# A block-matching convolution kernel: cosine transform on sixteen 32x32 tiles, its loads in pieces over the slots, products behind six multiply-adds, and another slot for layer 1's matmuls

## The chip, the cores and the metric

The kernel runs on one core of a Trainium2 chip. The metric is the device time of one execution in microseconds (us); less is better. In the profiles PE is TensorE's matmul side and PEld its weight loads, DVE is VectorE, ACT is ScalarE, POOL is GpSimd, and SP is the engine whose queue issues some of the DMAs. PSUM is the memory that matmuls write to, in banks of 128 partitions by 512 floats.

## The reference

The input is `x`, 8 images of 32 channels by 128x128 in float32. Two layers follow each other; `_gn` normalises over groups of channels.

```python
# layer 0, on x0 = _gn(x)
xb = _patch_match_stack(x0)      # for each pixel the 8 best of 25 shifts of x0
                                 # (5x5 window, 3x3 patch costs, top_k): [B, 256, H, W]
dct = _conv(xb, dct_w, groups=C) # 1x1, per channel 8 -> 8 maps: the "cosine transform"
h = jax.nn.relu(_conv(_conv(xb, w1), w2, groups=CK, pad=1))  # 1x1 over 256, 3x3 depthwise
h = jax.nn.relu(_conv(_conv(h, w3), w4, groups=CK, pad=1))
wiener = jax.nn.sigmoid(_conv(_conv(h, w5), w6, groups=CK, pad=1))
filt = _conv(wiener * dct, inv_dct_w, groups=C)
x = x + _conv(filt, agg_w)       # 256 -> 32
# layer 1: one 5x5 kernel for all channels
x = x + conv5x5(_gn(x), kernel)
```

The 256 maps are held as two tensors of 128 partitions by 8 rows by 128 columns. The inverse transform and `agg_w` are one matmul in the kernel (`pa`).

## The kernel before, in words

**Steps and slots.** An image is cut into 17 steps of up to 8 rows; the 8 images make 136 steps in one long pipeline. The main loop (L1056 on) goes through four *slots* a step, `i` = 3, 2, 1, 0. Slot `i` = 1, 2, 3 runs the i-th of layer 0's three "1x1, then 3x3 depthwise" blocks, each for another step (`si = s - (i - 1)`, block 3 two steps behind block 1). Slot 0 ends a step: the cosine transform, and its products with the sigmoid's result.

**A block.** Half of the 256 maps goes the "v" way and half the "t" way. `pointwise_v` (L658) multiplies 128-row groups into PSUM tiles `pv` (matmul L670), ScalarE copies them to `tv`. `depthwise_v` (L711) then makes the 3x3 convolution on DVE: ScalarE writes the first tap (L722), DVE does eight multiply-adds (L725), each 128x1024, and ScalarE the relu or the sigmoid (L729). `pointwise_t` (L680; matmuls `p`, L694; copies L701) and `depthwise_t` (matmuls `pw`, L751, ScalarE L764) do the same for the other half on TensorE, with the taps as banded matrices.

**The gather.** The 8 shifted copies of a pixel are gathered by matmuls: POOL loads the chosen places `ib` (L602) and the image's rows `xt` (L591), ScalarE turns the places into selection matrices `sel` (L616, L617), and TensorE multiplies (`gather_pixels`, `pg`, L631). ScalarE copies the result to `xb` (L638), the input of block 1. Each slot gathers a quarter of the step. After the last quarter of a step, POOL stores all of `xb` to DRAM as `xbd` (one DMA of 1 MB, L640), since the transform needs it two steps later.

**The end of a step.** `final_load` (L770), called at the end of slot 0 for the next step, has POOL load the input's rows `xr` (L781) and the stored maps `xf` (eight DMAs, L791). `final_dct` (L796) runs in slot 0: per half of the 8 rows, four matmuls of 64x64 tiles `pc` (L810) into two PSUM tiles, and two products on DVE, `acc = acc * pc` (L818). `ldct`, the weights of the transform, is made once at the start by `mixes` (L300): SP loads `dq` by 32 small DMAs (L308), and DVE multiplies it by a mask (L318). `final_add` (L820) follows in slot 0 and the next step's slot 3: matmuls `pa` (L831), an addition on DVE (L839), statistics (L840), and four POOL stores to `x1d` (L844).

**The other work.** While image b runs through the pipeline, image b+1 is prepared (patch costs: differences `df` L444, squares on ScalarE L452, sums over channels `pd` on TensorE L459, POOL's stores and loads `sq` L474 and `dsum` L492/L499, sums on DVE from L508 on, the eight best places by `mx` and `idx` L536/L537; the gather's table: `xl` L411, then `xtd`, 32 POOL stores L424/L429), and image b-1 goes through layer 1 (`layer1` L848: `xy` loads, normalisation, matmuls `p` of the 5x5 bands L924, additions L936, stores L938). These tasks are generators. Each `yield` names a queue (D: DVE, B, A, P: TensorE matmuls, Q), a cost and a number of slots to wait; the main loop calls `run("P")`, `run("Q")`, `run("A")` at fixed places of each slot, and `tick` runs D with a credit, 40% of a step's in slot 0 and 20% in each of the others.

**What sets the order.** The order of TensorE, DVE and ScalarE is written by hand: instructions run on each of them as the loop issues them (`manual_schedule`). The order on POOL and SP is the framework's, so an edit can move POOL's DMAs beyond what its lines say. `ps_x` holds five PSUM banks that `pv`, `p`, `pg`, `pc`, `pa`, `p` of layer 1 and others take in turn; `pd` and `pw` have pools of their own. `xf` has one buffer.

**The iterators of the main loop.** `depthwise_v` is a generator: its first part is ScalarE's first tap, its second the eight multiply-adds (`next(new_v)`, in the block's own slot), its third the activation (`next(dv)`, in the slot after it), its last the copy of the two overlapping rows (`next(kept)`, two slots later). `dt` goes through `depthwise_t` likewise. Slot 0 comes after block 1's slot 1, so on DVE the products L818 stand behind block 1's eight multiply-adds.

Of the kernel before, what the change touches and what calls it, by code (L numbers as in the profile page):

```python
# [16 lines left out]
P = 128  # L17
# [3 lines left out]
R = 8  # L21
# [23 lines left out]
def bm3d_conv_preact(  # L45
# [58 lines left out]
    lw5 = const.tile([P, 2, CK], F32, name="lw5")  # L104


    ldct = const.tile([P, 2, 64], F32, name="ldct")
    lagg = const.tile([P, 2, C], F32, name="lagg")


# [90 lines left out]

    queues = {"B": deque(), "D": deque(), "A": deque(), "P": deque(), "Q": deque()}

    PAIR = 1.95
    pairs = [0]
# [91 lines left out]

    def mixes():  # L300

        dq = work.tile([P, 2, K], F32, name="dq", tag="dq", bufs=1)
        src = dct_w.rearrange("(m h c i) k a b -> m h k c (i a b)", m=2, h=2, i=K)
        for k in range(K):
            for m in range(2):
                for h in range(2):
                    p = 64 * h + 32 * (k % 2) + 8 * (k // 2)
                    nc.sync.dma_start(dq[p : p + 8, m], src[m, (h + m + 1) % 2, k])  # L308
        m8 = work.tile([P, 8], F32, name="m8", tag="m16", bufs=1)
        yield "D", 1.0, 10  # L310
        nc.vector.tensor_reduce(
            m8,
            cst[:, C_M32 : C_M32 + C].rearrange("p (a c) -> p c a", c=8),
            axis=mybir.AxisListType.X,
            op=ALU.add,
        )
        for m in range(2):
            nc.vector.tensor_tensor(  # L318
                ldct[:, m].rearrange("p (c i) -> p c i", i=K),
                m8.unsqueeze(2).to_broadcast([P, 8, K]),  # L320
                dq[:, m].unsqueeze(1).to_broadcast([P, 8, K]),
                ALU.mult,
            )

        iv = work.tile([P, 2, K], F32, name="iv", tag="iv", bufs=1)
        nc.sync.dma_start(iv, inv_w.rearrange("(m p) k a b -> p m (k a b)", p=P))
        ag = work.tile([C, CK], F32, name="ag", tag="xr")
        nc.sync.dma_start(ag, agg_w.rearrange("c i a b -> c (i a b)"))
        for m in range(2):
            yield "D", 0.5  # L330
            ib = work.tile([P, P], F32, name=f"ib_{m}", tag="xm")
            nc.vector.tensor_tensor(
                ib.rearrange("p (c k) -> p c k", k=K),
                cst[:, C_M16 : C_M16 + 16].unsqueeze(2).to_broadcast([P, 16, K]),
                iv[:, m].unsqueeze(1).to_broadcast([P, 16, K]),
                ALU.mult,
            )
            yield "P", 0
            ps = ps_x.tile([P, 512], F32, name=f"ps_ag_{m}", tag="x")[:, :C]
            nc.tensor.transpose(ps, ag[:, m * P : (m + 1) * P], ident[:C, :C])  # L340
            agt = work.tile([P, C], F32, name=f"agt_{m}", tag="agt")
            nc.scalar.copy(agt, ps)
            yield "P", 0
            ps2 = ps_x.tile([P, 512], F32, name=f"ps_ia_{m}", tag="x")[:, :C]
            nc.tensor.matmul(ps2, ib, agt, start=True, stop=True)
            nc.scalar.copy(lagg[:, m], ps2)
# [273 lines left out]
    def gather_pixels(b, s4, f):  # L620

        n, h = s4 // 2, s4 % 2
        if h == 0 and f == 0:
            xbs[b, n] = xbp.tile([P, 2, R, W], F32, name=f"xb_{b}_{n}", tag="xb")
        xb, xt = xbs[b, n], xts[b, s4]
        sels = [selss.pop((b, s4, f, k2)) for k2 in range(2)]
        pg = ps_x.tile([P, 2, 4, HW], F32, name=f"pg_{b}_{s4}_{f}", tag="x")
        for t in range(NT // 2):
            xa, xz = TW * t, min(TW * (t + 1), HW)
            for j in range(4):  # L630
                nc.tensor.matmul(  # L631
                    pg[C * j : C * (j + 1), :, :, xa:xz],
                    xt[: 8 * QW, f * (NT // 2) + t],
                    sels[j // 2][: 8 * QW, j % 2 * 2 : j % 2 * 2 + 2, :, xa:xz],
                    start=True,
                    stop=True,
                )
        nc.scalar.copy(xb[:, :, 4 * h : 4 * h + 4, HW * f : HW * (f + 1)], pg)  # L638
        if h == 1 and f == 1:
            nc.gpsimd.dma_start(xbd[b][:, :, R * n : R * (n + 1)], xb)  # L640

# [67 lines left out]
    def depthwise_v(i, b, n):  # L711
        v = tv[i - 1]
        nr = R if n < NS else i
        out_ = accp.tile([P, R, W], F32, name=f"acc{i}_{b}_{n}_1", tag=f"acc{i}1")
        acc = out_[:, :nr]
        for k, (dy, dx) in enumerate(
            ((1, 1), (0, 0), (0, 1), (0, 2), (1, 0), (1, 2), (2, 0), (2, 1), (2, 2))
        ):
            tap = dwv[:, i - 1, 3 * dy + dx : 3 * dy + dx + 1]
            rows = v[:, dy : dy + nr, dx : dx + W]  # L720
            if k == 0:
                nc.scalar.activation(acc, rows, AF.Copy, scale=tap)  # L722
                yield out_
            else:
                nc.vector.scalar_tensor_tensor(  # L725
                    acc, rows, tap, acc, op0=ALU.mult, op1=ALU.add
                )
        yield
        nc.scalar.activation(acc, acc, funcs[i - 1])  # L729
        yield  # L730
        rows_before_v(i, b, n)
# [38 lines left out]
    def final_load(b, n):  # L770
        j0, j1 = (3, R) if n == 0 else (0, R if n < NS else 3)
        ya, yz = R * n - 3 + j0, R * n - 3 + j1

        whole = j1 - j0 == R
        nr, nw = (2, W) if whole else (j1 - j0, C)
        xr = work.tile([P, 2 * W], F32, name=f"xr_{b}_{n}", tag="xr")
        xr = xr[:, : nr * nw].rearrange("p (r w) -> p r w", w=nw)
        for j in range(4):
            ra = ya + 2 * j if whole else ya
            xa = 0 if whole else C * j  # L780
            nc.gpsimd.dma_start(  # L781
                xr[C * j : C * (j + 1)], x[b, :, ra : ra + nr, xa : xa + nw]
            )

        xf = xbp.tile([P, 2, R, W], F32, name=f"xf_{b}_{n}", tag="xf", bufs=1)
        src = xbd[b].rearrange("(j m h c) g y x -> g m h j c y x", j=4, m=2, h=2)
        for m in range(2):
            for h in range(2):
                for g in range(2):
                    p = 64 * h + C * g  # L790
                    nc.gpsimd.dma_start(  # L791
                        xf[p : p + C, m, j0:j1], src[g, m, (h + m + 1) % 2, :, :, ya:yz]
                    )
        return xr, xf, j0, j1

    def final_dct(b, n, acc, xf, j0, j1):  # L796

        for r0 in range(0, R, 4):
            a, z = max(r0, j0), min(r0 + 4, j1)
            if a >= z:  # L800
                continue


            pc = [
                ps_x.tile([P, 4, W], F32, name=f"pc_{b}_{n}_{m}_{r0}", tag="x") for m in range(2)
            ]
            for h in range(2):
                for m in range(2):
                    o = 64 * ((h + m + 1) % 2)
                    nc.tensor.matmul(  # L810
                        pc[m][o : o + 64, : z - a],
                        ldct[64 * h : 64 * h + 64, m],
                        xf[64 * h : 64 * h + 64, m, a:z],
                        start=True,
                        stop=True,
                    )
            for m in range(2):
                nc.vector.tensor_mul(acc[m][:, a:z], acc[m][:, a:z], pc[m][:, : z - a])  # L818

    def final_add(b, n, acc, xr, j0, j1):  # L820

# [26 lines left out]
    def layer1(b):  # L848
# [60 lines left out]
        for c in range(0, C, 8):  # L909
            if c == 0 or not last:  # L910
                yield "D", 2.0, 1 if last else 3
                normalise(c)
            yield "P", 0
            ps = [
                ps_x.tile([P, 4, W], F32, name=f"p5_{b}_{c}_{e}", tag="x") for e in range(2)
            ]
# [107 lines left out]
    def turn(credit):  # L1024
# [2 lines left out]
        run("B")  # L1027
        run("A")
        run("P")
        run("Q")  # L1030

    def until(cond, credit):
# [3 lines left out]
    with tc.manual_schedule(engines=ORDERED):  # L1036
        push(prep(0))
        push(weights())
        push(mixes())
        xbd[0] = dram.tile([P, 2, H, W], F32, name="xbd_0", tag="xbd")  # L1040
        for i in range(3):
            nc.gpsimd.memset(tb[i][0:64, 0], 0.0)
        for u in range(7):
# [12 lines left out]
        for s in range(len(steps) + 2):  # L1056
            if s < len(steps):
# [5 lines left out]
                    push(prep(b + 1))  # L1063
                if n == NS - 1 and b + 1 < NB:
                    until(lambda: b + 1 in ready, 4.0)
                    xbd[b + 1] = dram.tile([P, 2, H, W], F32, name=f"xbd_{b+1}", tag="xbd")
            for i in (3, 2, 1, 0):
                si = s - (i - 1 if i else 2)
                live = 0 <= si < len(steps)
# [4 lines left out]
                if live and i:  # L1074
                    src = source(i, bi, ni)
                    pointwise_v(i, bi, ni, lws[i - 1], src)
                    new_v, new_t = depthwise_v(i, bi, ni), depthwise_t(i, bi, ni)
                    accs[i, bi, ni] = [None, next(new_v)]
                next(later, None)
                if live and not i:  # L1080
                    if ni == 0:
# [3 lines left out]
                run("P")  # L1085
                if live and not i:
                    final_dct(bi, ni, accs[3, bi, ni], xf, j0, j1)

                run("Q")
                if s < len(steps):  # L1090
# [9 lines left out]
                    unit(gather_pixels, u)  # L1100
                next(dt, None)
                run("A")
                next(dv, None)
                if s < len(steps):
                    unit(gather_select, u + 1, (1,))
                    u += 1
# [2 lines left out]
                if live and not i:  # L1109
                    later = end(bi, ni, xr, j0, j1)  # L1110
                if not i and 0 <= s - 1 < len(steps):
                    fins[s - 1] = final_load(*steps[s - 1])
        next(kept, None)
        for _ in later:
            pass
# [63 lines left out]
```

## Time and profile before

| what | value |
|---|---|
| three runs | 6515.69, 6534.44 and 6527.66 us, median 6527.66 |
| the profiled execution | 6526.97 us, of which the span is 6525.2 |
| granted TensorE clock, mean | 0.979 |
| multiply-adds L725 | 3264, DVE busy 4031.6 us |
| depthwise matmuls `pw` L751 | 31680, PE busy 2118.1 us |
| transform `pc` L810 | 2112 records, PE busy 281.8 us |
| products L818 | 528, median 679 ns each |
| `xf` loads L791 | 1088, mean 632 ns to issue on POOL, median 6.6 us to landing |
| first and last `pc` | start at 287.9 and 6460.0 us |

A profile shows one execution: for each engine when it was busy, for each idle stretch which instruction ended it ("releaser"), and the chain of waits, followed from the last instruction back to whatever released each one. The start of `pc` marks the steps: there is one per step, and the time from one to the next is the step's length, 33 to 62 us.

### The profile page before, as it was taken

To read this page: it belongs to the slowest core of one execution; us is meant where nothing else is said; L and a number is where in the kernel's file an instruction comes from. 1 tells how busy PE (TensorE), PEld (TensorE's weight loads), DVE (VectorE), ACT (ScalarE), POOL (GpSimd) and SP (SyncE) were. 2 spreads that over 40 slices of the span, in tenths; PEclk is the share of its full clock that TensorE was granted. 3 is DMA by queue.
4 is the path that set the end of the run, shared out by engine and by line. 5 is a ranking of instruction groups with operands and counts; after the bars stand their busy time and mean duration, and the time that the engine had idled before them with its cause. 6 is when DMAs were issued, how large, how long until landed. Compare 5 with 4: busy or idle time off the path is not lost.

```text
span 6525.2 us, 234180 instructions
## 1 busy us (share of the span) xinstructions
PE 6180.3 (95%) x102306; PEld 3262.3 (50%) x102306; DVE 5856.5 (90%) x8828; ACT 5051.0 (77%) x6698; POOL 3077.3 (47%) x5015
## 2 busy tenths in 40 slices
PE   5799999999999999999999999999999999999997
PEld 1445445544555546454555544544545454465553
DVE  7899988999889998899998999899998999988776
ACT  5787769778787877877778787887869787787772
POOL 8345436444364444643446534454345644344334
PEclk7899999999999999999999999999999999999998
DMA  4555555565555655655546556565555665455553
GB/s 85 125 135 144 123 124 146 145 143 135 133 145 139 142 147 127 150 140 135 141 129 157 140 131 151 127 150 137 139 134 138 150 147 133 118 149 147 137 135 79
DMA packets 544960, 886.21 MB, mean 136 GB/s; under 512 B 248880, under 2 KB 312944, under 8 KB 543936
## 3 DMA queue, kind: packets, MB, share of 16 engines
q0 software_dynamic: 383648, 611.87, 37.4%
q1 hardware_dynamic: 157776, 258.11, 16.4%
q8 instruction: 805, 13.19, 0.9%
q10 hardware_dynamic: 2512, 1.25, 0.1%
q14 instruction: 219, 1.79, 0.1%
HBM read 420.60 MB, written 216.49 MB: 98 GB/s over the span
## 4 chain that ended last, share of the span: by engine, by line
PE 50%; DVE 32%; ACT 5%; POOL 5%; DMA 4%; issue 4%; SPq 0%; ACTq 0%; DVEq 0%; POOLq 0%
DVE acc L725 21%; PE pw L751 16%; PE pv L670 12%; PE p L694 11%; PE pg L631 4%; DVE idx L537 3%; POOL xtd L424 3%; PE pc L810 2%; DVE df L444 2%; DVE acc L818 1%; PE p L924 1%; DVE mx L536 1%; PE pd L459 1%; DMA t<-t 1%; ACT sel L616 1%
## 5 line engine op out<-in xcount | busy, mean ns | idle before, releaser
L725 DVE SCALAR_TENSOR_TENSOR acc<-tv,dwv,acc 128x1024 f32<-128x1024 f32 (+3 forms) x3264 | 4031.6, 1237 | 156.3 <-ACT acc L722 52.0
L751 PE MATMUL pw<-t,dwd 96*32 96x254 f32 (+7 forms) x31680 | 2118.1, 419 | 23.0 <-DMA t<-t 10.1
L751 PEld LDWEIGHTS pw<-t,dwd 96*32 96x32 f32 (+1 forms) x31680 | 1105.7, 110 | 826.8 <-issue 369.3
L616 ACT ACTIVATE sel<-ib,nplace 128x1024 f32<-128x1024 uint8 x1024 | 1170.8, 1143 | 62.0 <-DMA ib<-idxd 62.0
L617 ACT ACTIVATE sel<-sel 128x1024 f32<-128x1024 f32 x1024 | 1086.0, 1061 | 32.5
L670 PE MATMUL pv<-acc,lw 128*32 128x512 f32 x8448 | 959.8, 590 | 54.4 <-DVE acc L818 47.8
L694 PE MATMUL p<-acc,lw 128*32 128x256 f32 x16768 | 974.3, 379 | 2.2 <-issue 2.2
L602 POOL DMA_DIRECT2D ib<-idxd x512 | 292.0, 570 | 1207.3 <-ACT sel L616 1078.1
L791 POOL DMA_DIRECT2D xf<-xbd x1088 | 651.0, 632 | 279.9 <-PE pc L810 180.6
L694 PEld LDWEIGHTS p<-acc,lw 128*32 128x32 f32 x16768 | 570.7, 111 | 393.6 <-issue 67.4
L729 ACT ACTIVATE acc<-acc 128x1024 f32<-128x1024 f32 (+3 forms) x408 | 417.1, 1022 | 390.2 <-DVE acc L725 389.8
L678 ACT COPY tv<-pv 128x512 f32<-128x512 f32 (+2 forms) x784 | 435.9, 579 | 338.5 <-PE pv L670 334.1
L631 PE MATMUL pg<-sel,xt 120*32 120x88 f32 (+1 forms) x24576 | 611.7, 244 | 64.8 <-ACT sel L617 56.1
L631 PEld LDWEIGHTS pg<-sel,xt 120*32 120x32 f32 x24576 | 559.5, 111 | 219.2 <-ACT sel L617 74.4
L670 PEld LDWEIGHTS pv<-acc,lw 128*32 128x32 f32 x8448 | 290.2, 110 | 532.3 <-issue 409.7
L764 ACT ACTIVATE acc<-pw 128x512 f32<-128x512 f32 (+2 forms) x808 | 436.6, 572 | 133.4 <-PE pw L751 131.8
L444 DVE TENSOR_TENSOR df<-xn 128x786 f32<-128x786 f32 (+2 forms) x576 | 530.4, 972 | 2.2 <-PE pd L459 1.9
L701 ACT COPY t<-p 128x512 f32<-128x512 f32 x800 | 421.7, 571 | 115.4 <-PE p L694 115.4
L452 ACT ACTIVATE df<-df 128x786 f32<-128x786 f32 (+2 forms) x576 | 458.9, 859 | 50.0 <-DVE df L444 48.6
L722 ACT ACTIVATE acc<-tv,dwv 128x1024 f32<-128x1024 f32 (+3 forms) x408 | 455.1, 1115 | 42.3 <-PE pa L831 24.8
L670 PE MATMUL pv<-xb,lw 128*32 128x512 f32 x4096 | 470.8, 596 | 0.0
L694 PE MATMUL p<-xb,lw 128*32 128x256 f32 x8192 | 469.9, 380 | 0.0
(155 smaller groups left out, 5893.0 us busy)
## 6 DMA issues: line engine op xcount, KB each, us to landing
ib<-idxd POOLq DMA_DIRECT2D x512, 256.0 KB, 4.0
xbd<-xb POOLq DMA_DIRECT2D x128, 1024.0 KB, 6.0
xf<-xbd POOLq DMA_DIRECT2D x960, 128.0 KB, 6.8
t<-t SPq DMA_DIRECT2D x792, 128.0 KB
t<-t SPq DMA_DIRECT2D x384, 256.0 KB
tv<-tv SPq DMA_DIRECT2D x384, 130.0 KB
xt<-xtd POOLq DMA_DIRECT2D x240, 180.0 KB, 4.0
xtd<-xl POOLq DMA_DIRECT2D x192, 96.0 KB, 3.3
```

The lines of the kernel that those rows point to most:

```text
L444: nc.vector.tensor_sub(df[:, :, ca:cz], xn[:, r0 : r0 + SR, ca:cz], xn[:, r0 + dy : r0 + dy + SR, ca + dx : cz + dx],)
L452: nc.scalar.activation(df[:, :, ca:cz], df[:, :, ca:cz], AF.Square)
L616: nc.scalar.activation(sel, ib, AF.Square, bias=nplace)
L617: nc.scalar.activation(sel, sel, AF.Relu, scale=-1.0, bias=1.0)
L631: nc.tensor.matmul(pg[C * j : C * (j + 1), :, :, xa:xz], xt[: 8 * QW, f * (NT // 2) + t], sels[j // 2][: 8 * QW, j % 2 * 2 : j % 2 * 2 + 2 ...
L670: nc.tensor.matmul(ps[C * j : C * (j + 1), :hr], lhsT[:, g, P + C * j : P + C * (j + 1)], src(g)[:, h : h + hr], start=g == 0, stop=g == 1,)
L694: nc.tensor.matmul(ps[C * r : C * (r + 1), e, :nb], lhsT[:, g, s], rows[:, r : r + 4 * nb - 3 : 4], start=g == 0, stop=g == 1,)
L722: nc.scalar.activation(acc, rows, AF.Copy, scale=tap)
L725: nc.vector.scalar_tensor_tensor(acc, rows, tap, acc, op0=ALU.mult, op1=ALU.add)
L751: nc.tensor.matmul(pt[u][C * j : C * (j + 1), ka:kz, :nb, xa:xz], dwd[0:hi, i - 1, u, j, dx + 1], t[0:hi, j, ka:kz, :nb, xa + dx : xz + dx ...
L764: nc.scalar.activation(rows[:, u : u + 2 * nh[u] - 1 : 2, :nb], pt[u][:, : nh[u], :nb], funcs[i - 1])
L791: nc.gpsimd.dma_start(xf[p : p + C, m, j0:j1], src[g, m, (h + m + 1) % 2, :, :, ya:yz])
```

## The change

Five edits come together.

1. `final_dct` works on 32x32 tiles: for each of four parts `s` (a half `m` of the maps by a half of the rows) four matmuls, tile `q` writing to PSUM partitions of tile `(q+s) % 4`, so that 16 matmuls of different tiles follow each other and take four PSUM banks. The eight matmuls of 64x64 are gone, and all products come after all matmuls. `ldct` is 4x32 columns instead of 2x64.
2. `xbd` has the layout [256, H, W]. `gather_pixels` stores half of the rows after each second quarter, in four DMAs (eight a step instead of one). `final_load` becomes a generator: `xr` and the buffer first, then the load of `xf` in parts: part 0 at the end of slot 0, part 1 in slot 3, parts 2 and 3 in slot 2 (one DMA for part 0 and two for each other: seven a step instead of eight).
3. `mixes` loads `dq` in 64 DMAs of 8x8 floats, where it had 32.
4. Block 1's `depthwise_v` yields once more, before its seventh and eighth multiply-adds: in slot 0, `final_dct`'s products stand between the sixth and the seventh. The last two follow at once (`next(dv)`), and block 1's relu L729 goes to the next slot 3 (`next(kept)` after `pointwise_v`).
5. `layer1` puts its matmuls `p` L924 into a new queue "L", which the main loop runs at the place of the transform, but only in slots 3, 2 and 1 (and in slot 0 where no transform is due).

In the built program POOL has 5748 DMAs where it had 5020, TensorE 1056 more matmuls, and of the four groups of layer 1's matmuls of an image the third moves from ahead of `pc` to the following slot 3, and the fourth from slot 3 to slot 2. The order on POOL around the building of `xtd` (seven times, in step 5 of the first image and step 1 of the next six) changes as well: part 0 of `xf` is issued ahead of the 32 `xtd`, and then come `xbd`, `ib`, `x1d`, the 13 `dsum`, part 1, `xt`, `ib`, `xbd`, and parts 2 and 3.

```diff
-    ldct = const.tile([P, 2, 64], F32, name="ldct")
+    ldct = const.tile([P, 4, C], F32, name="ldct")
...
-        dq = work.tile([P, 2, K], F32, name="dq", tag="dq", bufs=1)
-        src = dct_w.rearrange("(m h c i) k a b -> m h k c (i a b)", m=2, h=2, i=K)
-        for k in range(K):
-            for m in range(2):
-                for h in range(2):
-                    p = 64 * h + 32 * (k % 2) + 8 * (k // 2)
-                    nc.sync.dma_start(dq[p : p + 8, m], src[m, (h + m + 1) % 2, k])
+        dq = work.tile([P, 4, K], F32, name="dq", tag="dq", bufs=1)
+        src = dct_w.rearrange("(m q c i) k a b -> m q c k (i a b)", m=2, q=4, i=K)
+        for s in range(4):
+            for q in range(4):
+                for c in range(4):
+                    p = C * q + K * c
+                    nc.sync.dma_start(dq[p : p + K, s], src[s // 2, (q + s) % 4, c])
...
-        if h == 1 and f == 1:
-            nc.gpsimd.dma_start(xbd[b][:, :, R * n : R * (n + 1)], xb)
+        if f == 1:
+            for j in range(4):
+                nc.gpsimd.dma_start(
+                    xbd[b].rearrange("(c j g) y x -> j c g y x", j=4, g=2)[
+                        j, :, :, 4 * s4 : 4 * s4 + 4
+                    ],
+                    xb[C * j : C * (j + 1), :, 4 * h : 4 * h + 4],
+                )
...
+                if i == 1 and k == 7:
+                    yield
                 nc.vector.scalar_tensor_tensor(
                     acc, rows, tap, acc, op0=ALU.mult, op1=ALU.add
                 )
...
-        src = xbd[b].rearrange("(j m h c) g y x -> g m h j c y x", j=4, m=2, h=2)
-        for m in range(2):
-            for h in range(2):
-                for g in range(2):
-                    p = 64 * h + C * g
+        yield xr, xf, j0, j1
+        src = xbd[b].rearrange("(m p) y x -> m p y x", m=2)
+        for s in range(4):
+            if s:
+                yield
+            m, r0 = s // 2, s % 2 * 4
+            a, z = max(r0, j0), min(r0 + 4, j1)
+            for pa, pz, at in ((0, P - C * s, C * s), (P - C * s, P, 0)):
+                if a < z and pa < pz:
                     nc.gpsimd.dma_start(
-                        xf[p : p + C, m, j0:j1], src[g, m, (h + m + 1) % 2, :, :, ya:yz]
+                        xf[pa:pz, m, a:z],
+                        src[m, at : at + pz - pa, R * n - 3 + a : R * n - 3 + z],
                     )
-        return xr, xf, j0, j1
+        yield
...
+        parts = [(s, max(s % 2 * 4, j0), min(s % 2 * 4 + 4, j1)) for s in range(4)]
+        parts = [(s, a, z) for s, a, z in parts if a < z]
+        pc = {
+            s: ps_x.tile([P, 4, W], F32, name=f"pc_{b}_{n}_{s}", tag="x") for s, a, z in parts
+        }
+        for s, a, z in parts:
+            for q in range(4):
+                o = C * ((q + s) % 4)
+                nc.tensor.matmul(
+                    pc[s][o : o + C, : z - a],
+                    ldct[C * q : C * (q + 1), s],
+                    xf[C * q : C * (q + 1), s // 2, a:z],
+                    start=True,
+                    stop=True,
+                )
+        for s, a, z in parts:
+            m = s // 2
+            nc.vector.tensor_mul(acc[m][:, a:z], acc[m][:, a:z], pc[s][:, : z - a])
...
-            yield "P", 0
+            yield "L", 0
...
+                if i == 3:
+                    next(kept, None)
                 next(later, None)
...
                     final_dct(bi, ni, accs[3, bi, ni], xf, j0, j1)
+                else:
+                    run("L")
+                if not i:
+                    next(dv, None)
...
-                next(dv, None)
+                if i:
+                    next(dv, None)
...
-                    fins[s - 1] = final_load(*steps[s - 1])
+                    loads = final_load(*steps[s - 1])
+                    fins[s - 1] = next(loads)
+                if 0 <= s - (1 if not i else 2) < len(steps):
+                    for _ in range({0: 1, 3: 1, 2: 2, 1: 0}[i]):
+                        next(loads)
```

## The prediction on record

> **What bounds the kernel now.** I read the page's first part and the chain of waits, then cut the trace into the steps of eight rows (from one `pc` to the next) and asked the windows view for them. By the first part TensorE (PE) is busy nearly always. The chain says that this is not the whole answer:
>
> ```profile
> PE 6180.3 (95%) x102306; PEld 3262.3 (50%) x102306; DVE 5856.5 (90%) x8828; ACT 5051.0 (77%) x6698; POOL 3077.3 (47%) x5015
> ...
> PE 50%; DVE 32%; ACT 5%; POOL 5%; DMA 4%; issue 4%; SPq 0%; ACTq 0%; DVEq 0%; POOLq 0%
> DVE acc L725 21%; PE pw L751 16%; PE pv L670 12%; PE p L694 11%; PE pg L631 4%; DVE idx L537 3%; POOL xtd L424 3%; PE pc L810 2%; DVE df L444 2%; DVE acc L818 1%; PE p L924 1%; DVE mx L536 1%; PE pd L459 1%; DMA t<-t 1%; ACT sel L616 1%
> ```
>
> PE sets the end for half of the span and VectorE (DVE) for a third; the transform `pc`, which the change shortens, has 2% of the chain (113.7 us when I add its links). Now three steps by the windows view (stretch, its length, busy time of PE, PEld, DVE, ACT, POOL, then the granted clock):
>
> ```profile
> 2678.80:2727.30 48.50, 47.34 (x807) 22.97 (x806) 42.58 (x46) 38.72 (x53) 41.70 (x58) 1.00 0.66 161
> 3129.60:3173.60 44.00, 44.00 (x767) 21.96 (x766) 42.50 (x87) 36.12 (x49) 21.31 (x36) 1.00 0.62 147
> 6135.80:6178.60 42.80, 42.80 (x756) 23.09 (x752) 33.99 (x31) 34.94 (x44) 11.99 (x23) 1.00 0.50 135
> ```
>
> The last is PE's own: 42.80 of 42.80 us, DVE 8.8 us idle. In the second PE is full and DVE idles only 1.5 us, so a shorter PE soon meets DVE. The first is step 0 of an image, with POOL 41.7 of 48.5 us busy: there POOL rebuilds the next image's gather table.
>
> **The transform, 8 tiles of 64x64 to 16 of 32x32.** One step's `pc` in PE's timeline (start, us):
>
> ```profile
> 3218.05 1.95 PE L810 MATMUL pc<-xf,ldct 64*64 64x512 f32 x16
> ...
> 3231.54 2.87 PE L670 MATMUL pv<-acc,lw 128*32 128x512 f32 x16 [3.59 <-DVE acc L818]
> ```
>
> The 16 records are 8 matmuls: two groups of four tiles, 0.97 us each. The new form has as many columns to stream per tile, but all 16 tiles can be one group: 1.95 - 0.97 = 0.98 saved, less 8 more instructions at 24 ns (the `pg` row: 48 records in 1.14 us) = 0.1 if these don't overlap. I take 0.88, with ends 0.5 and 0.95. It counts only where PE sets the pace. By the chain: 113.7 x 0.88/1.88 = 53. By steps: in images 1 to 6 PE idles little while DVE has 2 us or more to spare in steps 0, 3, 4, 5, 10, 12, 13, 16: 8 x 0.88 = 7 an image, 42 in six; the first image gives about 6, the last, where no next image is prepared, 11. I take **-59**, ends -25 (only the steps without a PE wait and with 4 us of DVE idle) and -70.
>
> The one group takes four of the five PSUM buffers at once; today the second group already needs buffers three and four before a product has freed the first, so the waits for buffers (32.7 us in 21 behind ScalarE's `t` copies) stay: 0, ends -10 and +10.
>
> The tiles of a group share PSUM banks. In the trace, two row halves write one bank at different partitions, and the 8 matmuls still take 1.95 us where four pairs in turn would take 4 x 0.97 = 3.9; I therefore let all 16 run together.
>
> The Trainium skill, page "TensorEngine Tiling (Array Packing)", section "Gotcha 1: PSUM Pressure", speaks against it: tiles in different rows can't access the same PSUM bank at the same time. By that rule each step would take 3.9 us in place of 1.95; the row here disagrees.
>
> **The products behind six multiply-adds.** They finish two multiply-adds (2 x 1.28 us) earlier. The wait shown above, 3.59 us of `pv` for a product, is one of 28 that sum to 47.8 us. They lie in steps 8, 10 and 11, where DVE idles only 1.4 to 4.4 us: DVE's work in the step stays, so a wait that goes is met later at another DVE result. I take 0 in steps 8 and 11; the 1.5 of step 10 is inside the 59. A product can now meet a late `pc`: DVE idled 10.5 us in all for it, ends -10 and +10. The relu of layer 1 moves to the next slot on ScalarE, where it waits 389.8 us in all for DVE and holds nobody: 0.
>
> **Layer 1's matmuls out of the transform's slot.** Two of each image's four groups (4.48 us each) move one slot. PE's sum stays. Their adds on DVE keep their row: 0, ends -10 and +10 (DVE waits of 4 to 8 us for `p` L924 in step 5 can shrink or grow).
>
> **More DMAs on POOL.** A step's `xb` store becomes 8 pieces, the transform's load 7 instead of 8 but spread over four slots; 728 issues of 0.63 us are 459 us on an engine that is 47% busy. DVE's 1.284 us a multiply-add is the same in steps with POOL idle and full, so it costs DVE nothing. What counts is the last issue before `pc`. In all ordinary steps the load's issue has 9.6 to 38 us to spare: 0. In the seven steps where the table is built it has not. POOL there, now:
>
> ```profile
> 2686.57 24.62 POOL L424 DMA_DIRECT2D xtd<-xl  x30 [0.88 <-DMA xl<-xs]
> ...
> 2714.86 0.75 POOL L640 DMA_DIRECT2D xbd<-xb  x1
> 2715.48 1.31 POOL L791 DMA_DIRECT2D xf<-xbd  x2
> 2717.58 2.26 POOL L791 DMA_DIRECT2D xf<-xbd  x4 [0.78 <-DMA xtd<-xl]
> 2719.83 0.59 POOL L602 DMA_DIRECT2D ib<-idxd  x1
> ...
> 2728.81 5.29 POOL L499 DMA_DIRECT2D dsum<-sq  x9 [0.53 <-DMA x1d<-xr]
> ```
>
> 24.6 us of table stores, then `xf`, landed at 2726.4, then `pc`:
>
> ```profile
> 2727.27 1.09 PE L810 MATMUL pc<-xf,ldct 64*64 64x512 f32 x8
> ...
> 2736.65 1.09 PE L631 MATMUL pg<-sel,xt 120*32 120x88 f32 x40 [2.22 <-ACT sel L617]
> ...
> 2737.75 6.87 PE L751 MATMUL pw<-t,dwd 96*32 96x256 f32 x94
> ```
>
> In the changed program POOL has only part 0 of the load ahead of the table; parts 1 to 3 come after the four `x1d` stores, the 13 `dsum` and another four `xbd`. By durations of these rows: table ends 2712.3, `xbd` x4 2716.1, `ib` 2716.7, `x1d` 2718.8, `dsum` 2726.6, part 1 2727.9, `xt` and `ib` 2729, `xbd` x4 2731.8, parts 2 and 3 2734.3, landed 5 us later at 2739.5. `pc` then starts 12 us late. Not all of that is lost: before, PE waited at `sel` until 2736.65 for the `ib` behind the loads, which now comes 3.7 us sooner, so `pg`, `pd` and the like run first. From the late `pc`: 0.9 + 1.4 (`pd`) + 1.0 (`pg`), so `pw` starts at 2742.6 instead of 2737.75: +4.9. The granted clock is .83 in the 10 us after today's wait, and a longer wait adds about 2 by that ratio: **+7 a place, 7 places: +49**. Ends: 3 (the loads slip through) and 14 (`dsum` wait for `x1d`, as they do now, and nothing is made up). The first image's place gives 4.9 by the same sum, image 1's 4.3.
>
> **The constants' load.** SP issues 32 tiny loads of `dq`, and `ldct` on DVE uses them:
>
> ```profile
> 23.40 23.00 SPq L308 DMA_DIRECT2D dq<-in_L_conv_dct_w_dram  x32
> ```
> ```profile
> 53.55 0.40 DVE L318 TENSOR_TENSOR ldct<-m,dq 128x64 f32<-128x64 f32 x2
> ```
>
> 64 at 0.715 us end at 69.1, landing 1.9 later: 71.0. DVE stands there from 53.55, 17.5 us, with all of `df` queued behind; ScalarE's squares follow `df`, and the `xs` copies that POOL needs are queued behind those on ScalarE. POOL's chain to the table stalls about 15 (from 60.7 to 76), and the first `pc` at 287.9 shifts as much: **+15**, ends 10 and 18.
>
> **Sum.** The profiled execution took 6526.97 us (span 6525.2), the runs' median is 6527.66, so I start from 6527: 6527 - 59 + 15 + 49 = **6532**. What a measurement of this kernel can tell from no change is about 0.3%, 19.6 us: 6508 to 6547 is "same".
>
> **Rivals.**
>
> *Faster:* the late pieces cost 2 a place (PE has `pg`, `pd`, `pw` of other units to run): 6527 - 59 + 15 + 14 = 6497. For it: written order lets `pg` run before `pc`. Against: POOL is 41.7 of 48.5 us busy there. Chance 0.22.
>
> *Slower:* the same pieces, full price. One mechanism: parts 1 to 3 of the load stand behind table and `dsum` on POOL; from 12 us at each of 7 places on it decides. 6527 - 50 + 15 + 98 = 6590. For it: `dsum` has waited for `x1d` here, and DVE, which wants `dsum` next, is late too (+6.1 by the same sum). Chance 0.27.
>
> *Not 16 at once:* `pc` takes 3.9 us. 130 steps x 1.95 = 254; with +64 for start and places 6845, or 6718 if it costs only in half the steps. The 1.95 us row speaks against it. Chance 0.06.
>
> *Nearly cancels*, 6532, own range 6510 to 6550: chance 0.45.
>
> **Chances.** Faster: 0.21 of the first rival and 0.06 of the likeliest: 0.27. Same: 0.01, 0.02 of the second and 0.31: 0.34. Slower: 0.25, 0.06 and 0.08: 0.39. The range goes to both first rivals with some room, 6480 to 6595.
>
> **What would show it.** `pc` 1.0 us a step in one group (right) or 3.9 (wrong); the first `pc` near 303; at seven places a PE wait of some 10 us for the DMA `xf` before `pc`; PE waits for the product nearly gone, DVE's idle in steps 6 to 9 unchanged. If steps 12 and 13 (39.9 and 35.0 us, PE only) don't shrink by 0.9, the gain is wrong; if the seven places keep their length, the loss is.

## The result and the profile after

The changed kernel takes 6539.07 us (median of 12 runs, 6525.9 to 6549.56); the kernel before, run beside it, 6523.24 (12 runs). The ratio is 1.0022, 95% interval 1.0014 to 1.0029: 14 us slower, within the 0.3% that the prediction called the same, and inside the likeliest case's own range (6510 to 6550, forecast 6532). The sum came out nearly right; three of its terms did not. The profiled execution, at 6530.17 us (span 6528.4), lies below that median, so losses are read from it step by step and sized by the runs.

The page of the changed kernel, its first and fourth part, to be held against the lines shown of before:

```profile
PE 6129.3 (94%) x104418; PEld 3332.3 (51%) x104418; DVE 5849.1 (90%) x8830; ACT 5046.5 (77%) x6698; POOL 3385.5 (52%) x5743
...
PE 44%; DVE 32%; ACT 10%; POOL 6%; DMA 4%; issue 4%; SPq 0%; ACTq 0%; DVEq 0%; POOLq 0%
DVE acc L733 21%; PE pw L759 16%; PE pv L676 10%; PE p L700 9%; DVE idx L537 3%; PE pg L631 3%; POOL xtd L424 3%; ACT sel L616 2%; PE p L934 2%; DVE df L444 2%; ACT df L452 2%; PE pc L819 1%; DVE acc L828 1%; DVE mx L536 1%; PE pd L459 1%
```

PE is busy 51 us less, as meant, and yet the span is no shorter: its share of the chain fell from 50% to 44%, and ScalarE's rose from 5% to 10%. TensorE got less work and waits more. In PE's timeline the transform itself (start, duration in us, instruction, number of records; below, brackets give the idle time ahead of it and what ended it):

```profile
3225.83 1.33 PE L819 MATMUL pc<-xf,ldct 32*32 32x512 f32 x32
```

One group now, 1.33 us where it was 1.95: the 32 records (16 matmuls of two records each, four matmuls to a bank) start within 0.74 us and are given some 0.6 us each. The saving is 0.62, not 0.88. The windows view, for step 1 of image 3, step 4 of image 4 and step 7 of the last image (columns as before, the granted clock is the third number from the end):

```profile
2734.77:2798.61 63.84, 56.42 (x839) 27.99 (x838) 51.91 (x81) 42.58 (x55) 38.44 (x64) 0.89 0.63 160
3681.46:3742.29 60.83, 53.64 (x839) 25.02 (x835) 51.33 (x63) 41.36 (x54) 34.11 (x53) 0.92 0.55 137
6146.74:6188.90 42.16, 42.16 (x775) 23.45 (x771) 34.00 (x31) 34.61 (x44) 15.16 (x29) 1.00 0.51 139
```

The last is the pure PE step: 42.78 before, 42.16 now, exactly the 0.62. The other two are the losses. Step 1 of image 3, with the table of the next image, was 57.7 us; step 4 of image 4 was 46.8. In both PE is idle over 7 us, and the granted clock falls to 0.89 and 0.92 around the waits.

**Step 1.** PE's timeline from the transform on:

```profile
2734.77 1.06 PE L819 MATMUL pc<-xf,ldct 32*32 32x512 f32 x8
2740.09 2.01 PE L819 MATMUL pc<-xf,ldct 32*32 32x512 f32 x8 [4.27 <-DMA xf<-xbd]
2745.23 4.40 PE L819 MATMUL pc<-xf,ldct 32*32 32x512 f32 x16 [3.13 <-DMA xf<-xbd]
2749.56 2.52 PE L459 MATMUL pd<-df,neg 128*32 128x393 f32 x16
2751.91 1.12 PE L631 MATMUL pg<-sel,xt 120*32 120x88 f32 x48
2752.85 5.34 PE L759 MATMUL pw<-t,dwd 96*32 96x256 f32 x96
```

Part 0 is there, part 1 keeps PE waiting, then parts 2 and 3. From `pc` to `pw` it was 10.5 us and is 18.1. POOL's timeline says why:

```profile
2695.97 24.61 POOL L424 DMA_DIRECT2D xtd<-xl  x30 [2.13 <-DMA xl<-xs]
...
2728.36 0.69 POOL L492 DMA_DIRECT2D dsum<-sq  x1
2729.04 3.05 POOL L499 DMA_DIRECT2D dsum<-sq  x5
2732.62 4.11 POOL L499 DMA_DIRECT2D dsum<-sq  x7 [0.54 <-issue]
2736.73 1.06 POOL L803 DMA_DIRECT2D xf<-xbd  x2
...
2741.53 2.06 POOL L803 DMA_DIRECT2D xf<-xbd  x4
```

POOL is hardly ever idle between these (over the whole step before, it is busy for 89 to 94% of the time at the seven places): the pieces stand in a queue behind `dsum`, and part 1 isn't even issued when `pc` begins.

**Step 4**, image 4, PE's timeline before:

```profile
3674.03 4.48 PE L924 MATMUL p<-xm,band 64*64 64x512 f32 x40
3678.33 1.88 PE L810 MATMUL pc<-xf,ldct 64*64 64x512 f32 x10
...
3692.27 0.44 PE L569 MATMUL pi<-cst,oc 128*128 128x128 f32 x2
```

In the changed kernel, PE's timeline, then DVE's:

```profile
3692.29 1.04 PE L841 MATMUL pa<-acc,lagg 128*32 128x256 f32 x16
3696.24 0.41 PE L569 MATMUL pi<-cst,oc 128*128 128x128 f32 x2 [2.91 <-DVE oc L560]
3696.58 6.18 PE L934 MATMUL p<-xm,band 64*64 64x512 f32 x40
...
3715.66 1.55 PE L459 MATMUL pd<-df,neg 128*32 128x396 f32 x8 [4.28 <-ACT sm L470]
```
```profile
3702.81 1.28 DVE L946 TENSOR_TENSOR xy<-xy,p 128x512 f32<-128x512 f32 x2 [3.16 <-PE p L934]
...
3734.04 7.89 DVE L733 SCALAR_TENSOR_TENSOR acc<-tv,dwv,acc 128x1024 f32<-128x1024 f32 x6 [4.74 <-ACT acc L728]
```

Before, the third group of layer 1's matmuls (L924) stood ahead of `pc`, at the end of step 3, and `pi` didn't wait. Now the group (L934) stands behind `pi`, which waits for DVE's `oc`, and DVE's own additions wait for it in turn. Steps 3 and 4 of images 1 to 6 went from 49.6 + 48.4 us to 44.2 + 60.4.

### The profile page after: what moved, and what is told of

It reads as the page before. It is cut to its first block, busy times and chain, and to the rows that moved or that the text cites. A ratio compares the mean times of both kernels' runs of the same rounds, so it can differ in the third digit from the quotient of the medians.

```text
span 6528.4 us, 239337 instructions
## 1 busy us (share of the span) xinstructions
PE 6129.3 (94%) x104418; PEld 3332.3 (51%) x104418; DVE 5849.1 (90%) x8830; ACT 5046.5 (77%) x6698; POOL 3385.5 (52%) x5743
## 4 chain that ended last, share of the span: by engine, by line
PE 44%; DVE 32%; ACT 10%; POOL 6%; DMA 4%; issue 4%; SPq 0%; ACTq 0%; DVEq 0%; POOLq 0%
DVE acc L733 21%; PE pw L759 16%; PE pv L676 10%; PE p L700 9%; DVE idx L537 3%; PE pg L631 3%; POOL xtd L424 3%; ACT sel L616 2%; PE p L934 2%; DVE df L444 2%; ACT df L452 2%; PE pc L819 1%; DVE acc L828 1%; DVE mx L536 1%; PE pd L459 1%
## 5 line engine op out<-in xcount | busy, mean ns | idle before, releaser
L759 PE MATMUL pw<-t,dwd 128*32 128x254 f32 (+7 forms) x31680 | 2111.8, 418 | 16.5 <-DMA t<-t 7.3
L759 PEld LDWEIGHTS pw<-t,dwd 96*32 96x32 f32 (+1 forms) x31680 | 1119.9, 110 | 799.6 <-issue 365.5
L700 PE MATMUL p<-acc,lw 128*32 128x256 f32 x16768 | 989.9, 382 | 0.0
L700 PEld LDWEIGHTS p<-acc,lw 128*32 128x32 f32 x16768 | 609.4, 111 | 364.8 <-issue 71.1
L602 POOL DMA_DIRECT2D ib<-idxd x512 | 309.3, 604 | 726.1 <-ACT sel L616 685.8
L641 POOL DMA_DIRECT2D xbd<-xb x1024 | 550.3, 544 | 257.8 <-ACT xb L638 171.1
L803 POOL DMA_DIRECT2D xf<-xbd x920 | 481.1, 529 | 369.2 <-PE pc L819 332.6
L854 POOL DMA_DIRECT2D x1d<-xr x544 | 274.0, 510 | 526.9 <-DVE xr L849 494.3
```

The costliest lines, as they stand in the source:

```text
L641: nc.gpsimd.dma_start(xbd[b].rearrange("(c j g) y x -> j c g y x", j=4, g=2)[j, :, :, 4 * s4 : 4 * s4 + 4], xb[C * j : C * (j + 1), :, 4 * ...
L700: nc.tensor.matmul(ps[C * r : C * (r + 1), e, :nb], lhsT[:, g, s], rows[:, r : r + 4 * nb - 3 : 4], start=g == 0, stop=g == 1,)
L759: nc.tensor.matmul(pt[u][C * j : C * (j + 1), ka:kz, :nb, xa:xz], dwd[0:hi, i - 1, u, j, dx + 1], t[0:hi, j, ka:kz, :nb, xa + dx : xz + dx ...
L803: nc.gpsimd.dma_start(xf[pa:pz, m, a:z], src[m, at : at + pz - pa, R * n - 3 + a : R * n - 3 + z],)
```

## The experiments

All times are medians of device time; ratios are to the kernel before, run on the same chip. Step lengths are means over images 1 to 6, from each run's trace.

| run | us | ratio (95%) | step 1 | steps 3 + 4 |
|---|---|---|---|---|
| the kernel before (beside rows 2 to 5, 6 to 9, 10 to 12) | 6523.74, 6526.2, 6524.62 | 1 | 59.0 | 98.0 |
| the changed kernel, again | 6540.28 | 1.0023 (1.0014 to 1.0032) | 62.9 | 104.4 |
| layer 1 in P | 6523.46 | 0.9999 (0.9990 to 1.0008) | 63.1 | 95.4 |
| loads in slot 0 | 6489.9 | 0.9949 (0.9936 to 0.9963) | 55.9 | 105.3 |
| products behind eight | 6542.7 | 1.0029 (1.0018 to 1.0039) | 62.7 | 105.4 |
| loads in slot 0, and P | 6484.08 | 0.9940 (0.9926 to 0.9954) | 56.5 | 97.6 |
| and products behind eight: transform alone | 6493.95 | 0.9947 (0.9935 to 0.9960) | 59.2 | 97.5 |
| loads in slot 0 on SP, and P | 6457.47 | 0.9899 (0.9885 to 0.9914) | 54.5 | 95.2 |
| loads in slot 0, third group in P | 6465.61 | 0.9908 (0.9893 to 0.9924) | 57.0 | 96.6 |
| loads in slot 0 on SP, third group in P | 6430.19 | 0.9855 (0.9841 to 0.9869) | 54.8 | 96.3 |
| loads spread on SP, third group in P | 6432.26 | 0.9861 (0.9846 to 0.9876) | 55.1 | 96.7 |
| the kernel before, loads on SP | 6576.03 | 1.0089 (1.0075 to 1.0102) | 55.4 | 98.9 |

**The changed kernel again.** No edit.

> The changed kernel once more, unedited, as the yardstick for the other runs and to see how far two profiles of it agree. The changed kernel's runs lay between 6525.9 and 6549.6 us (median 6539), 1.0022 of the kernel before. Expected: a ratio of 1.001 to 1.003, and the same step lengths within 0.3 us in steps 6 to 13 of images 1 to 6; if the lengths of steps 1 to 4 differ by several us from one profile to the other, single profiles there are worth less than sums over six images.

The ratio repeats. Steps 6 to 13 agree within 0.4 us, steps 3 and 4 within 0.8, and the wait for `xf` before `pc` is 46.5 us in this profile and 45.8 in the first: the mean step lengths below are more than chance where they differ by over 1 us. A single step can differ by 2 (step 4 of the last image: 44.0 and 46.1).

**Layer 1 in P.**

```diff
-            yield "L", 0
+            yield "P", 0
```

> The changed kernel with layer 1's matmuls back in queue P, so the third group of an image stands ahead of pc again. Theory A: the queue L moves 4.5 us of TensorE work that had filled the time in which TensorE is ahead of VectorE (end of step 3) to behind pi L569, which waits for VectorE's oc in step 4; TensorE then stalls for oc and sm, and VectorE's add of p and its first tap come late. Steps 3 and 4 of images 1 to 6 went from 49.6 + 48.4 to 44.2 + 60.4 us, so undoing the move should give about 50 + 47: 7 to 8 us an image less, 40 to 47 in six, some 3 given back in image 7. Expected 6495 to 6505, ratio about 0.996. Rival B: the stalls of step 4 come from the products and the relu that moved on VectorE and ScalarE; then the time stays within 8 us of the changed kernel.

17 us less, with an interval that lies apart from the control's, but not 40. Theory A holds for the place: steps 3 and 4 together go from 104.4 to 95.4, 54 us in six images. It fails for the sum: step 2 got 2.6 longer and step 7 3.3, as if the work that the stalls held up had been paid in step 4 and is paid there now; the last image takes some back as well. Over steps 1 to 11 the idle time falls little, VectorE's from 35 us an image to 33 and TensorE's from 25 to 23 (added from the traces). What holds the rest wasn't tried by itself.

**Loads in slot 0.**

```diff
-                    for _ in range({0: 1, 3: 1, 2: 2, 1: 0}[i]):
+                    for _ in range({0: 4, 3: 0, 2: 0, 1: 0}[i]):
```

> The changed kernel with all four parts of the xf load issued at the end of slot 0, as before the change (still in 7 DMAs); on POOL parts 1 to 3 then stand behind the table's stores but ahead of x1d and dsum. Theory A: TensorE's wait of 6 to 7 us for xf in step 1 (step 5 of image 0) goes; step 1 shrinks from 62.6 by 3 to 6 us, of which step 2 takes back up to 2. Expected 10 to 28 us less in all, 6511 to 6529. Rival B: what waits for xf now waits for ib and sel as it did before the change, and step 2 gives back the rest: within 8 us of the changed kernel.

50 us less, twice what I expected, and what the prediction had charged: 49. Step 1 loses 7.0 us in six images (42), step 5 of the first image 6.8. PE's long waits for `xf` are gone. POOL's timeline at the same place of image 3, with the loads now ahead of `x1d` and `dsum`:

```profile
2699.78 3.08 POOL L803 DMA_DIRECT2D xf<-xbd  x6
2702.85 0.58 POOL L602 DMA_DIRECT2D ib<-idxd  x1
2703.42 2.33 POOL L854 DMA_DIRECT2D x1d<-xr  x4
2706.66 0.69 POOL L492 DMA_DIRECT2D dsum<-sq  x1 [0.90 <-DMA xf<-xbd]
```

I had set the lower figure because step 1 had grown by only 3.6 us against the kernel before. That comparison hid half of the cost: without the late pieces step 1 is 3.1 us shorter than before. The two runs below that differ by the products alone (both undone, and the transform alone: 56.5 and 59.2) put most of that on the products behind six multiply-adds; there, step 2 gives 2.3 of it back.

**Products behind eight.** The `yield` before `k == 7` is out, and `next(dv)` and `next(kept)` are back at their old places.

```diff
-                if i == 1 and k == 7:
-                    yield
```

> The changed kernel with the products behind all eight multiply-adds of block 1 again, and its relu back in slot 0. Theory A: the earlier products took away TensorE's waits for them in steps 7 to 11; steps 7 and 8 became 3.0 us shorter each, steps 9 and 11 2.4 and 1.1 longer, so undoing costs 3 to 4 us an image, 18 to 25 in six: 6555 to 6565. Rival B: VectorE has no time to spare there, so what TensorE loses for the products it wins elsewhere: within 8 us of the changed kernel. Rival C: the earlier products made the stalls of step 4: 30 to 45 us less.

Rival B: 2.4 us, inside the noise. PE's wait of `pv` for the product comes back, 57.6 us in 30 against 23.2 in 8 (waits view), and the time doesn't care: step 8 is 3.6 us longer, step 9 2.8 shorter. That fits Rival B's reason, PE waiting for DVE here, for this result or for the next.

**Both undone.** The two edits of the second and third experiment together.

> Both undone: all parts of the xf load at the end of slot 0, and layer 1's matmuls in queue P. The transform on 16 tiles and the products behind six multiply-adds stay. Alone, the loads in slot 0 took 50 us off the changed kernel and queue P 17. Theory A, two causes at different places (step 1, and steps 2 to 7): they add up, 6540 - 50 - 17 = 6473, ratio about 0.992. Rival B: with step 1 short, TensorE is no longer late in steps 2 to 4 and the loss by the queue is another one: 6480 to 6500, as with the loads alone.

They don't add up: 6484, 6 us from the loads alone, and the intervals overlap. That is Rival B in size; the trace shows steps 3 and 4 at 97.6 in place of 105.3 (46 us in six images), given back in part in steps 2 and 7 (2.7 and 3.2 longer) and in steps 3 to 5 of the last image (5.8 together).

**The transform alone.** Both undone, and the edit of the fourth as well.

> As the run with both undone, and the products behind all eight multiply-adds with the relu in slot 0: what is left of the change is the transform on 16 tiles, its loads in 7 DMAs at the old place, and the stores in 8 pieces. Theory A: pc takes 1.33 us where it took 1.95, and 0.62 on the steps where TensorE sets the pace (some 80 of 135) is 50: 6474, within 5 us of the run with both undone, since the products behind six brought 2 us in the changed kernel. Rival B: the products behind six are worth 15 to 20 us where nothing else stalls step 4: 6490.

The time is Rival B's, 20 us above what theory A asked for; but to the run with the products behind six it is only +10 us, and those two intervals overlap, as in the changed kernel. So the theory is wrong in its other half: the transform with its loads and stores brings 5.3 thousandths, 35 us (interval 26 to 42), less than the 50 that 80 steps at 0.62 would give. Not every step in which PE looked like the pacemaker passes the gain on.

**Loads on SP.** Both undone, and the loads of `xf` on another queue:

```diff
-                    nc.gpsimd.dma_start(
+                    nc.sync.dma_start(
                         xf[pa:pz, m, a:z],
```

> As the run with both undone, but the seven xf loads are issued on SP's queue, so that they stand behind nothing of POOL's. If POOL's queue is what the loads wait for at the seven table steps (theory A), TensorE's wait for xf there goes to nothing and ib and dsum come 4 us sooner: 5 to 20 us less than with both undone. Rival B: SP is in order too, and the load waits there for the last pc to free xf, with the copies of t and tv queued behind it: steps get longer everywhere, 20 us or more slower.

27 us less than with POOL's queue, more than theory A's 5 to 20, and nothing of Rival B: the pure PE steps of the last image keep their 42.1. But theory A has the place only in part. In the run with both undone PE's waits view has no wait for `xf` left to win. ScalarE's waits for `ib` do fall, from 40.7 us to 18.1 in the whole run, as the theory's second half has it. But between the two profiled executions, which lie 46 us apart, step 1 brings only 12 us in six images (56.5 to 54.5); steps 4 and 7 bring 12 and 10, and the last image 6. POOL's order is another one in this run (the four big loads `xn` of the next image come in steps 9 and 10 where they came in 9, 10 and 11), so how much is the shorter queue and how much the new order isn't separated.

**Third group in P.** Loads in slot 0 on POOL, and

```diff
-            yield "L", 0
+            yield "P" if c == 16 else "L", 0
```

> The loads in slot 0, queue L kept for three of the four groups of layer 1, and only the third (c = 16, the one that fell behind pi in step 4) back in queue P. Theory A: the third group's place is the whole loss of the queue, so step 4 is back at 46 to 48 us and step 3 at 49; the time is that of the run with both undone within 5 us (6473). Rival B: the loss comes from the fourth group in step 5 or from all; then the time stays at the 6490 of the loads alone.

6466, better than either queue for all groups (6490 and 6484). The third group's place is what hurts: steps 3 and 4 are at 96.6, and step 2 keeps the 48.0 that queue L gives it. The other groups gain by L: against all in P, step 2 is shorter by 16 us in six images; in the last image step 4 gains 5.1 and step 5 gives 2.2 back.

**Both, with the loads on SP; and spread again.** The last two edits together, once with all parts in slot 0 and once with the changed kernel's spreading.

> The xf loads on SP's queue, all at the end of slot 0, and of layer 1's matmuls only the third group back in queue P; all else as changed. With both queues in P the loads on SP gave 6457, and keeping the other three groups in L gave 18 us more than all in P with the loads on POOL (6466 to 6484). Theory A: two different places, they add up: 6435 to 6445, ratio about 0.987. Rival B: the 18 us came from steps 4 and 5 of a late POOL queue that is not late any more: 6450 to 6460.

> As the run before it, but with the parts of the load spread over slots 0, 3, 2 as in the changed kernel, still on SP. Theory A: the spreading in itself costs nothing, only the place on POOL's queue behind table and dsum did: within 8 us of the run before it. Rival B: the late parts arrive late from SP too: 20 to 50 us more.

6430 and 6432: these effects add up (6439 was the plain sum, 9 us more, which the intervals cover), and both runs are faster than both kernels, the first by 1.45% of before. The spreading costs nothing once the queue isn't POOL's. One step's load on SP, in the spread version:

```profile
6138.41 4.68 SPq L803 DMA_DIRECT2D xf<-xbd  x7
```

**The kernel before with its loads on SP.**

> The kernel before the change with nothing but its eight xf loads issued on SP. If POOL's queue at the seven table steps is what costs there already (TensorE idles 4.9 us in step 1, by the trace), 15 to 30 us less than before, 6495 to 6510, and the gain of the SP queue is independent of the transform. Rival B: before the change, the loads stood ahead of x1d and dsum and were not what step 1 waited for: 6520 to 6530.

Both theories miss: 51 us slower. Step 1 does fall, from 59.0 to 55.4, so the POOL queue cost there before the change as well. But step 10 grows from 45.3 to 53.1. PE's timeline in image 3, then POOL's:

```profile
3206.30 2.76 PE L751 MATMUL pw<-t,dwd 96*32 96x256 f32 x48
3218.46 5.32 PE L751 MATMUL pw<-t,dwd 96*32 96x256 f32 x48 [9.39 <-issue]
```
```profile
3199.31 0.86 POOL L87 DMA_DIRECT2D xn<-in_x_dram  x1 [1.72 <-issue]
...
3204.34 0.87 POOL L87 DMA_DIRECT2D xn<-in_x_dram  x1
```

`pw` stops half way. The profile names nothing for this wait; the other half of its input are copies `t`, which SP had issued at 3207.1 and 3207.6, and in the whole run `pw` waits 55.0 us in 25 for such copies (10.1 in 6 before). Two of the next image's four big loads `xn` (608 or 560 KB each) are now issued just before them, 18 to 30 us into step 10; before, POOL issued its last three at 37 and 44 us into step 10 and in step 11, and in the spread version on SP the last two at 38 and 43 us into step 10. So POOL's order was planned anew when the loads left it. The trace speaks for `xn` as the reason. In image 6, which has no `xn` to load any more, step 10 keeps its 45.8 us; in image 2, where the two loads come latest, at 25 and 30 us into the step, it grows by 1.0, and in images 1, 3, 4 and 5 by 7 to 14. The windows view of the stretch from 24 to 36 us into step 10, image 3 and then image 6 (behind the granted clock stands the mean busy share of the DMA engines):

```profile
3204.10:3216.10 12.00, 4.97 (x124) 3.05 (x116) 11.75 (x11) 6.48 (x8) 2.21 (x4) 0.92 1.01 163
5587.10:5599.10 12.00, 12.00 (x220) 6.23 (x216) 11.75 (x11) 9.03 (x13) 4.94 (x10) 1.00 0.47 124
```

With `xn` in flight the DMA engines are full (1.01) and `pw` goes on 11 us after its copies' issue; without it they are half busy (0.47) and PE is never idle. No run moved `xn` alone, so the cause is argued from these times, not tested.

## Why the prediction came out right, point by point

- **The transform** (-59): the mechanism is right, 16 tiles in one group with four to a bank. The term was mis-sized: 0.62 us a step instead of 0.88, and -35 in all (the transform alone). Steps 12 and 13 of images 1 to 6, which were to shrink by 0.9 if the gain was right, shrink by 0.2 to 0.5. The trace's start times say where the 0.26 us went. In the old form the two records of a tile start 0.43 to 0.48 us apart and the last is given 0.59, so that one group of four alone is about 1.07 us, not half of 1.95. And in the new form (the step of 3225.83) the records start in fours, the fourth four 0.27 us after the first, where the estimate allowed 0.1 for it. 1.07 + 0.27 is 1.34; 1.33 was measured. This is a reading of two traces, since no other group size was run.
- **The banks**: right. The first eight of those records start within 0.05 us and are given 0.61 us each, so they run side by side; by the order of issue all four tiles of the first bank are among them. The Trainium skill, page "TensorEngine Tiling (Array Packing)", section "Gotcha 1: PSUM Pressure", would have tiles of different rows not access one bank at a time; this trace differs, 1.33 us for all.
- **The products** (0): right, for the reason given. The waits for the product halved (47.8 us to 23.2, not "nearly gone"), and nothing came of it in the changed kernel. With both other edits undone the products bring 10 us, but the intervals overlap.
- **Layer 1's queue** (0, ends -10 and +10): wrong, +17 in the changed kernel. The step that failed is "their adds on DVE keep their row": DVE's order indeed stayed, but the third group moved past `pc` and behind `pi`, an instruction that waits for DVE. I counted the work that moved and not what it was moved behind.
- **The late loads** (+49): right in the mechanism, 7 us a place and 50 in all by the run that takes them away (38 in the pair with queue P). The order on POOL is as worked out; PE waits for `xf` 6.5 us a place on the mean (45.8 in all), where some 10 were forecast, and the first `pw` of step 1 starts 16.2 us after `pc` where it was 11.1 (means of six): +5.1, where the sum had 4.9. That the total is 49 has luck in it: against the kernel before, step 1 is only 3.6 to 3.9 us longer, and the other 3.1 of the 7 are a gain, put mostly on the products above, that the late pieces hide and that the prediction had at 0.
- **The constants** (+15): wrong, +1 to +3. The first `pc` is at 290.6 in the first profile and 289.3 in the second, after 287.9. SP:

```profile
23.58 23.67 SPq L308 DMA_DIRECT2D dq<-in_L_conv_dct_w_dram  x64
```

  64 loads take as long as 32 did, 0.37 us each instead of 0.715. Each has 64 floats for 8 partitions as before, but they now lie side by side in DRAM, where they lay 8 floats apart. The duration of a row was measured for one form of load, and I carried it to another; that the addresses are the reason was not tried by itself.
- **The sum.** With loads and queue both undone, the kernel is 42 us faster than before (6526.2 to 6484.08; 39 by the ratio): that is what transform, products and start bring, where the prediction had -44. The loads and the queue add 56 to it, where it had 49. The sum is +14, near the measured +14 to +17. Inside the first figure, a gain that was too large stood against a start that was too dear; in the second, 50 and 17 overlap by some 10. That two such pairs fell together is luck; that late pieces would eat the transform's gain is not.
- **The rivals.** *Faster*, 6497, was met in size by the run without late loads (6490); *slower*, at 14 us a place, was twice too dear (and its sum takes the transform at -50, where the forecast had -59); *not 16 at once* is out, by 1.33 us against 3.9.

## What to carry to other kernels

When loads are cut into pieces and spread in the program, look where each piece lands on its queue: the last piece sets the arrival, and here a queue that is 52% busy on the mean was 89 to 94% busy in just the seven steps that count. Before moving matmuls out of an engine's crowded slot, look at what they pass: here the same matmuls filled time in which TensorE was ahead, and behind an instruction that waits they held up two engines. And take an effect from the run that undoes it, not from the step lengths of before and after alone, where other edits of the same change cover it.

## What the runs showed of the hardware

- DMA loads of 64 floats to 8 partitions each, on SP's queue, took 0.715 us apiece where the floats lay 8 apart in DRAM (32 loads) and 0.37 us where they lay side by side (64 loads).
- A piece of the `xf` load takes POOL 0.526 us to issue in the changed kernel, and SP 0.469 in the spread version (medians of 920).
- Storing `xb` in eight pieces of 128 KB in place of one of 1 MB: each lands 3.6 us after its issue (median, changed kernel), where the whole took 6.0.
- The 32 records of one `pc` group start in fours at 0, 0.03, 0.13 and 0.27 us, and again 0.43 to 0.46 us after each of these. What sets the 0.13 and 0.27 is open; it wasn't tried.
